# A Mamba scan on Trainium2: the product with C written one column to the left of the states, and the carried state copied later by ScalarE instead of GpSimd

## Chip, core and metric

The kernel runs on one core of one Trainium2 chip. The metric is the device time of one execution in microseconds (us); lower is better. The engines are named as in the profile: PE is TensorE's matmul, PEld its weight load, DVE is VectorE, ACT is ScalarE, POOL is GpSimd, and SP is SyncE, whose queue issues the DMAs.

## What is computed

The input `x` is 8 samples of 512 channels by 48 x 48 = 2304 positions. Layer 0 is a causal linear attention with 8 heads, layer 1 splits the 512 channels into four blocks of 128 and runs a Mamba block on each, one after the other, since block i gets the result of block i-1 added to its input. The change lies in the recurrence of the Mamba block:

```python
delta = softplus(dt @ Wdt.T + bdt)
A = -exp(A_log)                                   # 256 channels x 16 states
dA = exp(einsum('bld,dn->bldn', delta, A))
dBu = einsum('bld,bln->bldn', delta * xs, Bm)
def step(h, inp):
    dA_t, dBu_t, C_t = inp
    h = dA_t * h + dBu_t
    return (h, einsum('bdn,bn->bd', h, C_t))      # y_t = sum over the states of h * C
```

So for every channel and state there is a first-order recurrence along the 2304 positions, and the states are then multiplied by C and summed over the 16 states. Around it stand projections, a convolution over four positions, two gates with silu, a skip `xs * Dp`, and a fusion of input and output by maxima and means. Everything is in float32.

## The kernel before

**Tiling.** A sample's block is a *stream block*; it is cut along the positions into NC = 6 chunks of LC = 384. One chunk of one block is a `Job`; there are 192. Two streams, even and odd samples, take turns in the order of the list `turns`, so that one stream's block boundary falls beside the other's work. The 128 partitions hold 64 channels times two states. A job has eight *slots*: half of the channels (`h = s // 4`) times four pairs of states, and a slot has four scans of 384 columns each (`NG` = 2 state groups times 2 channel groups). There are 1536 slots.

**One slot.** All of a slot's data is in one tile `u` of shape 128 x 2 x 2 x 385, out of five that go round (`bufs=5`). In each of its four rows, column 0 takes the state carried in from the chunk before, and columns 1 to 384 hold first the products B times `delta * xs` and then, in place, the states. The steps, with the lines that the profile names:

- `last_product` (L856, POOL) takes a tile `u` and writes the products of its last 128 columns; ahead of it ScalarE copies the carried state from `state` into column 0 (L855). It is issued at the middle of a slot for the slot two later.
- `product` (L867, DVE) writes the first 256 columns from `dxp`, a copy in PSUM that `inputs` (L840, ACT) makes. It is issued at a slot's start for the next slot.
- `decay` (L877, ACT) writes `exp(delta * A)` into a PSUM bank. Decays run up to `DEPTH` = 3 ahead of the scans; six banks are shared with the attention and the projections.
- `scan` (L888, DVE) runs the recurrence on one row of `u`, in place, and frees the decay's bank.
- `weigh` (L902 and L904, POOL), after the four scans: it first copies the last column, that is the state to be carried to the next chunk, into the small tile `state` (not in the last chunk, hence 1280 times), and then multiplies columns 1 to 384 in place by C.
- `gather` (L911, PE) adds the products up over the states by four matmuls into `yp` in PSUM. It is issued at the middle of the slot after next, from the list `waiting`.
- `skip` (L845, ACT) writes `xs * Dp` into `yp` before a half's gathers, and `gated` (L923, DVE) multiplies the finished half by the gate into `yz`.

**What else the engines do.** The attention of the next samples (`chunk`: projections L293, features L305 and L306, `q` L350, `k` L358), the preparation of the next jobs (`prepare`: convolution L693, silu, softplus L764, `delta * xs` L805), statistics and the passing on of a block's result (`pass_on`: `fu` L662, `xi` L667, `xo` L670) run as *tasks* between the scans. `delta * xs` overwrites `delta` in place, so it waits until `delta` has been stored for the broadcast of `dr`.

**What sets the order.** The whole program is written under `manual_schedule`: each engine executes its instructions in the order in which the Python code issues them, and a wait at the head of an engine's queue holds everything behind it. Function `slot` issues a slot's work; its middle is the point after the second scan (`i == 1`). Tasks carry due times in half slots and are stepped by `beside`.

Of the kernel before, what the change touches and what calls it, by code (L numbers as in the profile page):

```python
# [12 lines left out]
ALU = mybir.AluOpType  # L13
# [4 lines left out]
P = 128  # L18
T = 128
LC = 384  # L20
NG = 2
# [29 lines left out]
def attention_then_mamba_kernel(  # L51
# [17 lines left out]
    nc = tc.nc  # L69
# [94 lines left out]
    def flush(every=True):  # L164
        while stores and (every or stores[0][0] <= half_no[0] - 2):
            _, o, i = stores.pop(0)
            nc.sync.dma_start(out=o, in_=i)
# [506 lines left out]
    class Job:  # L674
# [222 lines left out]

        def weigh(self, s, u):

            h, q = s // 4, s % 4 * NG  # L900
            if self.c + 1 < NC:
                nc.gpsimd.tensor_copy(self.state[:, h, q : q + NG, :], u[:, :, :, LC])  # L902
            h = u[:, :, :, 1:]
            nc.gpsimd.tensor_tensor(  # L904
                h, h, self.C[s % 4].unsqueeze(2).to_broadcast([P, NG, 2, LC]), ALU.mult
            )

        def gather(self, s, u):
            for j in range(NG):
                for g in range(2):  # L910
                    nc.tensor.matmul(  # L911
                        self.yp[g * 64 : g * 64 + 64, 0:LC],
                        pair_sum,
                        u[:, j, g, 1:],
                        start=False,
                        stop=(s % 4 == 3 and j == NG - 1),
                        skip_group_check=True,
                    )
# [96 lines left out]
    def finale(job):  # L1015
        yield "0", 1
        job.project()
        yield "1", 0
        job.maximum()
        if job.c == NC - 1:  # L1020
            yield from job.stream.pass_on()
# [29 lines left out]
    def beside(half):  # L1051

        half_no[0] = half
        flush(every=False)
        begin(half // 2 + LEAD)

        for t in heads:
            if t.need is not None and t.need[1] == 0 and t.fits() and t.due():
                t.step()
        held = False  # L1060
        for t in tasks + heads:
            while t.need is not None and t.due():
                if not t.fits() or held and t.need[1]:
                    held = held or t.need[1] > len(spare)
                    break
                t.step()
        prune()

    def hurry(k, ready):

        for _ in range(1000):
            flush()
            begin(k)
            if ready():
                break
            moved = False
            for t in heads + tasks:
                if t.need is not None and t.fits() and (t.start <= k and t in tasks or t.due()):
                    need = t.need
                    t.step()  # L1080
                    moved = moved or t.need != need or need[0] != "1w"
            if not moved:
                half_no[0] += 1
            prune()
        assert ready()

    def at(k):
        return jobs[k // SLOTS], k % SLOTS

    def apart(k):  # L1090

        return k % SLOTS == 0 and k > 0 and at(k)[0].c == 0 and at(k)[0].stream is at(k - 1)[0].stream

    us, decays, waiting = {}, [], []
    todo = 0
    primed, drawn = set(), set()

    def ahead(n):

        nonlocal todo  # L1100
        while len(decays) < n and spare and todo < 4 * slots:
            k = todo // 4
            if apart(k) and k not in primed:
                break
            job, s = at(k)
            if not job.prepared or s // 4 not in job.dr:
                break
            decays.append(job.decay(s, todo % 4))
            todo += 1

    def close(k):

        job = at(k)[0]
        while waiting:
            waiting.pop(0)()
        job.gated(1)
        job.closed = True
        tasks.insert(0, Task(finale(job)))

    def prime(k):  # L1120
        job, s = at(k)
        hurry(k, lambda: job.prepared)
        primed.add(k)
        job.inputs(0)
        for r in range(2):
            us[k + r] = job.last_product(s + r)
        job.product(s, us[k])
        ahead(DEPTH)

    def slot(k):  # L1130
        job, s = at(k)
        end = k + 1 == slots or apart(k + 1)
        if not end and k + 1 not in drawn:
            j, r = at(k + 1)
            j.product(r, us[k + 1])
        before = jobs[k // SLOTS - 1] if k >= SLOTS else None
        if s == 2 and before is not None and not before.closed:
            before.gated(1)
            tasks.insert(0, Task(finale(before)))
        elif s == 6:  # L1140
            job.gated(0)
        beside(2 * k)
        for i in range(4):
            job.scan(s, i, us[k], decays.pop(0))
            if i == 0 and s in (2, 6):
                job.skip(s // 4)
            ahead(DEPTH)
            if i == 1:

                if len(waiting) > 1:  # L1150
                    waiting.pop(0)()
                if s == 2:
                    job.inputs(1)
                elif s == 6 and k + 2 < slots and not apart(k + 2):
                    j = at(k + 2)[0]
                    if not j.prepared:
                        hurry(k + 2, lambda: j.prepared)
                    j.inputs(0)
                if not end and k + 2 < slots and not apart(k + 2):
                    j, r = at(k + 2)  # L1160
                    us[k + 2] = j.last_product(r)
                    if s == 7:

                        j.product(r, us[k + 2])
                        drawn.add(k + 2)
                beside(2 * k + 1)
        u = us[k]
        job.weigh(s, u)
        waiting.append(lambda: at(k)[0].gather(s, us.pop(k)))
        if end:  # L1170
            close(k)
            if k + 1 < slots:
                prime(k + 1)
            else:
                hurry(slots, lambda: not tasks)
                flush()

    with tc.manual_schedule():
        half_no[0] = FIRST - 6
        Task(statistics(0)).finish()  # L1180
        for st in streams:
            tasks.append(Task(st.weights()))
            tasks.append(Task(st.pass_on()))
        for half in range(FIRST - 6, 0):
            beside(half)
        prime(0)
        for k in range(slots):
            slot(k)
# [70 lines left out]
```

## Time and profile before

| | |
|---|---|
| Median of 3 runs | 8786.02 us (8785.19 to 8791.31) |
| Span of the profiled execution, first to last instruction | 8790.1 us; its time beyond the span is not listed apart |
| Instructions in the profile | 122,627 |
| Mean granted TensorE clock | 0.964 |
| DMA: share of 16 engines, rate | about 70%, mean 187 GB/s |
| POOL COPY `state<-u` (L902) | 1280 times, 242.4 us |
| POOL TENSOR_TENSOR `u<-u,C` (L904) | 1536 times, 4882.7 us, mean 3179 ns |
| DVE scans (L888) | 6144 times, 5457.0 us, mean 939 ns |
| ACT decays (L877) | 6144 times, 3413.6 us, mean 578 ns |

How to read it: the page's first part gives each engine's busy time and its share of the span. The costliest groups have, after the bar, the busy time of a group, the mean time of one instruction, and the idle time of the engine just before the group's instructions with what ended it. The waits say who waited for whom: total us, number of times, longest. The chain of waits follows the work that ended last back from the end, at each step to what released it. The timeline gives start and duration of each instruction in us; equal neighbours are merged ("x2").

### The profile page before, as it was taken

The numbers are of one execution on the slowest core, as the hardware profiler recorded it, in microseconds if no ns is written. First come the engines' busy times: TensorE is split into PE (matmuls) and PEld (weight loads), VectorE is DVE, ScalarE is ACT, GpSimd is POOL, SyncE is SP. The second block draws the span as 40 slices with busy tenths as digits, with TensorE's granted clock in tenths as the row PEclk, the third lists the DMA queues.
The fourth block names the chain that finished last, engine by engine and source line by source line (L and its number), as shares of the span: only waits on it lengthen the run. The fifth ranks groups of instructions, "written<-read, shape, count | busy, mean of one in ns | idle before, by whom it ended". The sixth has DMA issues, their size and how long they took to land.

```text
span 8790.1 us, 122627 instructions
## 1 busy us (share of the span) xinstructions
PE 7766.8 (88%) x36482; PEld 3705.4 (42%) x36482; DVE 8067.0 (92%) x11078; ACT 6744.5 (77%) x13220; POOL 8044.8 (92%) x5623
## 2 busy tenths in 40 slices
PE   7899999998899899998889999999888999999865
PEld 4444444444444444444444444444444444444422
DVE  2899999999899999998889999999889999999998
ACT  2777887777788878777778878877777888877875
POOL 1789999999999999999999999999999999999998
PEclk9999999999999999999999999999999999999977
DMA  5667777766676777776667677777667666766655
GB/s 184 166 174 189 193 197 195 190 188 186 190 191 188 191 195 198 196 190 189 179 190 192 188 191 198 198 195 188 188 183 191 189 187 187 189 187 185 183 156 144
DMA packets 1002907, 1642.98 MB, mean 187 GB/s; under 512 B 138592, under 2 KB 797312, under 8 KB 1002240
## 3 DMA queue, kind: packets, MB, share of 16 engines
q1 hardware_dynamic: 1002240, 1635.13, 69.0%
q8 instruction: 291, 4.77, 0.2%
q14 instruction: 376, 3.08, 0.1%
HBM read 1309.06 MB, written 325.58 MB: 186 GB/s over the span
## 4 chain that ended last, share of the span: by engine, by line
DVE 28%; POOL 20%; ACT 14%; DMA 13%; PE 13%; issue 7%; SPq 4%; POOLq 0%; DVEq 0%; ACTq 0%
DVE u L888 19%; POOL u L904 11%; ACT bank L877 5%; DVE u L867 5%; POOL u L856 4%; PE bank L693 4%; PE bank L293 3%; PE yp L911 3%; DMA C<-scr 3%; SPq L797 2%; DMA dscr<-delta 2%; ACT L877 2%; DMA B<-scr 1%; ACT L764 1%; POOL delta L805 1%
## 5 line engine op out<-in xcount | busy, mean ns | idle before, releaser
L888 DVE TENSOR_TENSOR_SCAN u<-bank,u 128x385 f32<-128x385 f32 (+1 forms) x6144 | 5457.0, 939 | 350.1 <-ACT bank L877 300.3
L904 POOL TENSOR_TENSOR u<-u,C 128x1536 f32<-128x1536 f32 x1536 | 4882.7, 3179 | 121.9 <-DVE gm_m L182 16.9
L877 ACT ACTIVATE bank<-dr,av 128x385 f32<-128x385 f32 (+1 forms) x6144 | 3413.6, 578 | 752.3 <-DVE u L888 611.9
L911 PE MATMUL yp<-u,cst 128*64 128x384 f32 x12288 | 2440.7, 519 | 428.2 <-POOL u L904 355.9
L856 POOL TENSOR_TENSOR u<-B,dxr 128x512 f32<-128x512 f32 x1536 | 1960.9, 1277 | 16.5 <-DMA dxr<-xscr 13.8
L867 DVE TENSOR_TENSOR u<-B,dxp 128x1024 f32<-128x1024 f32 x1536 | 1836.0, 1195 | 11.3 <-ACT dxp L840 11.1
L293 PE MATMUL bank<-xn,wq_sb 128*128 128x384 f32 x4608 | 1680.1, 508 | 82.2 <-POOL xn L317 40.1
L911 PEld LDWEIGHTS yp<-u,cst 128*64 128x64 f32 x12288 | 782.0, 140 | 1660.6 <-issue 842.6
L693 PE MATMUL bank<-xi,wk 128*128 128x384 f32 x3072 | 1117.8, 507 | 218.5 <-ACT kl L390 112.5
L293 PEld LDWEIGHTS bank<-xn,wq_sb 128*128 128x128 f32 x4608 | 849.0, 195 | 826.5 <-DVE u L888 119.6
L693 PEld LDWEIGHTS bank<-xi,wk 128*128 128x128 f32 x3072 | 560.6, 192 | 780.8 <-ACT kl L390 202.1
L805 POOL TENSOR_TENSOR delta<-delta,xs 128x384 f32<-128x384 f32 x384 | 384.4, 1001 | 278.0 <-DMA dscr<-delta 215.9
L305 ACT ACTIVATE ex<-bank,bqkv_sb 128x384 f32<-128x384 f32 x384 | 221.0, 576 | 523.8 <-PE bank L293 523.6
L877 ACT ACT_TABLE_LOAD x382 | 490.1, 1283 | 6.7
L845 ACT ACTIVATE yp<-xs,pv 128x384 f32<-128x384 f32 x384 | 223.8, 583 | 290.8 <-DVE yz L923 289.3
L902 POOL COPY state<-u 128x4 f32<-128x4 f32 x1280 | 242.4, 189 | 172.6 <-DVE u L888 170.0
L753 PE MATMUL bank<-dbc,wd 9*128 9x384 f32 x768 | 315.6, 532 | 1.2 <-ACT dbc L745 1.1
L929 PE MATMUL bank<-yz,wo 128*128 128x384 f32 x768 | 299.2, 506 | 18.5 <-DVE yz L923 14.6
L704 PE MATMUL bank<-xi,wi 128*128 128x384 f32 x768 | 285.9, 494 | 10.9 <-ACT xs L729 10.9
L740 PE MATMUL bank<-xs,wx 128*40 128x384 f32 x768 | 281.0, 489 | 2.6 <-ACT sm L457 2.6
L923 DVE TENSOR_TENSOR yz<-yp,sz 128x384 f32<-128x384 f32 x384 | 211.6, 551 | 62.5 <-PE yp L911 62.3
L423 PE MATMUL bank<-cst,rdb 128*128 128x128 f32 x576 | 113.0, 311 | 170.7 <-DVE u L888 168.5
(117 smaller groups left out, 8018.7 us busy)
## 6 DMA issues: line engine op xcount, KB each, us to landing
B<-scr SPq DMA_DIRECT2D x1536, 192.0 KB
C<-scr SPq DMA_DIRECT2D x1536, 192.0 KB
xn<-xn SPq DMA_DIRECT2D x192, 768.0 KB
dr<-dscr SPq DMA_DIRECT2D x768, 192.0 KB
dxr<-xscr SPq DMA_DIRECT2D x768, 192.0 KB
dscr<-delta SPq DMA_DIRECT2D x192, 384.0 KB
xscr<-delta SPq DMA_DIRECT2D x192, 384.0 KB
xn<-in_x SPq DMA_DIRECT2D x48, 768.0 KB
```

Source lines behind the costliest of these rows:

```text
L293: nc.tensor.matmul(ps, wq_sb[:, kt, j * 512 + o * P : j * 512 + (o + 1) * P], xn[:, kt, :], start=(kt == 0), stop=(kt == 3),)
L693: nc.tensor.matmul(xc, wk[:, k, h * P : (h + 1) * P], xi[:, c0 + k : c0 + k + LC], start=(k == 0), stop=(k == 3),)
L704: nc.tensor.matmul(zp, wi[:, 256 + h * P : 256 + (h + 1) * P], xi[:, c0 + 3 : c0 + 3 + LC], start=True, stop=True,)
L753: nc.tensor.matmul(vp, wd[32:41, h * P : (h + 1) * P], dbc[32:41, :], start=True, stop=True)
L805: nc.gpsimd.tensor_tensor(delta[:, h, :], delta[:, h, :], xs[:, h, :], ALU.mult)
L856: nc.gpsimd.tensor_tensor(u[:, :, :, 1 + LC - TAIL :], self.B[s % 4][:, :, cols].unsqueeze(2).to_broadcast(shape), self.dxr[s // 4][:, :, ...
L867: nc.vector.tensor_mul(u[:, :, :, 1 : 1 + LC - TAIL], self.B[s % 4][:, :, cols].unsqueeze(2).to_broadcast(shape), self.dxp.unsqueeze(1).to ...
L877: nc.scalar.activation(dA[:, cols], self.dr[h][:, g, cols], AF.Exp, scale=self.w[6][:, 2 * h + g, q + j : q + j + 1],)
L888: nc.vector.tensor_tensor_scan(u[:, j, g, cols], dA[:, cols], u[:, j, g, cols], 0.0, ALU.mult, ALU.add,)
L904: nc.gpsimd.tensor_tensor(h, h, self.C[s % 4].unsqueeze(2).to_broadcast([P, NG, 2, LC]), ALU.mult)
L911: nc.tensor.matmul(self.yp[g * 64 : g * 64 + 64, 0:LC], pair_sum, u[:, j, g, 1:], start=False, stop=(s % 4 == 3 and j == NG - 1), skip_gro ...
L929: nc.tensor.matmul(self.xm[:, 0:LC], self.w[2][:, h, :], self.yz[:, h, :], start=(h == 0), stop=(h == 1),)
```

## The change

Three things are changed. `weigh` still multiplies columns 1 to 384 by C, but writes the result to columns 0 to 383, so the last column keeps the raw state. `gather` reads from columns 0 to 383. The copy of the last column into `state` leaves `weigh` and GpSimd; it is a function of its own, `keep`, on ScalarE, put into a list `kept` at the end of a slot and issued at the middle of the next slot, ahead of everything else that is issued there (or in `close`, where a run of slots ends).

```diff
         def weigh(self, s, u):
 
+            nc.gpsimd.tensor_tensor(
+                u[:, :, :, 0:LC],
+                u[:, :, :, 1:],
+                self.C[s % 4].unsqueeze(2).to_broadcast([P, NG, 2, LC]),
+                ALU.mult,
+            )
+
+        def keep(self, s, u):
+
             h, q = s // 4, s % 4 * NG
             if self.c + 1 < NC:
-                nc.gpsimd.tensor_copy(self.state[:, h, q : q + NG, :], u[:, :, :, LC])
-            h = u[:, :, :, 1:]
-            nc.gpsimd.tensor_tensor(
-                h, h, self.C[s % 4].unsqueeze(2).to_broadcast([P, NG, 2, LC]), ALU.mult
-            )
+                nc.scalar.copy(self.state[:, h, q : q + NG, :], u[:, :, :, LC])
...
                         pair_sum,
-                        u[:, j, g, 1:],
+                        u[:, j, g, 0:LC],
                         start=False,
...
-    us, decays, waiting = {}, [], []
+    us, decays, waiting, kept = {}, [], [], []
...
     def close(k):
 
         job = at(k)[0]
+        while kept:
+            kept.pop(0)()
         while waiting:
             waiting.pop(0)()
...
             if i == 1:
 
+                while kept:
+                    kept.pop(0)()
                 if len(waiting) > 1:
                     waiting.pop(0)()
...
         job.weigh(s, u)
+        kept.append(lambda: at(k)[0].keep(s, u))
         waiting.append(lambda: at(k)[0].gather(s, us.pop(k)))
```

## Prediction

> **What bounds the kernel now.** I read the busy shares first, then the waits of each engine, then one job at a time, then the chain of waits. The busy line:
>
> ```profile
> PE 7766.8 (88%) x36482; PEld 3705.4 (42%) x36482; DVE 8067.0 (92%) x11078; ACT 6744.5 (77%) x13220; POOL 8044.8 (92%) x5623
> ```
>
> Two engines, DVE and POOL, are level, and each is idle for some 720 to 745 us of the span. Cut by jobs (eight slots), the stretches differ. In a quiet job both are almost full; in a disturbed one neither is. The windows of busy time (columns: us, then PE, PEld, DVE, ACT, POOL) of one job of each kind:
>
> ```profile
> 3177.00:3222.00 45.00, 38.97 (x190) 18.62 (x190) 42.43 (x58) 36.17 (x74) 39.38 (x31) 1.00 0.76 201
> 3313.40:3355.70 42.30, 39.12 (x194) 18.78 (x193) 41.77 (x57) 35.02 (x70) 41.03 (x29) 1.00 0.71 188
> ```
>
> The quiet job takes 42.3 us with 41.8 of DVE work: DVE sets it, and nothing done to POOL can shorten it. But POOL works 41.0 of the 42.3 us, so it has almost no reserve to catch up when something has held it. What holds it, and who waits later, is in the waits (us, times, longest):
>
> ```profile
> POOL delta L805 <- DMA dscr<-delta: 215.9, 93, 25.9
> POOL state L902 <- DVE u L888: 170.0, 152, 13.9
> ```
>
> ```profile
> DVE u L888 <- ACT bank L877: 300.3, 212, 4.4
> DVE q L350 <- ACT bank L306: 102.4, 57, 6.0
> DVE yz L923 <- PE yp L911: 62.3, 39, 6.6
> DVE u L888 <- POOL u L856: 49.0, 41, 2.9
> ```
>
> The second line of POOL's waits carries most: only 152 of 1280 state copies found POOL waiting for DVE's scans, so in the other 88% POOL was behind. Measured slot by slot in the timeline, `weigh` starts a median 2.55 us after the slot's last scan ends. The disturbed job shows the mechanism in POOL's timeline (start, us):
>
> ```profile
> 3190.09 1.27 POOL L856 TENSOR_TENSOR u<-B,dxr 128x512 f32<-128x512 f32 x1
> 3196.33 1.00 POOL L805 TENSOR_TENSOR delta<-delta,xs 128x384 f32<-128x384 f32 x1 [4.97 <-DMA dscr<-delta]
> 3197.28 0.18 POOL L902 COPY state<-u 128x4 f32<-128x4 f32 x1
> 3197.54 3.17 POOL L904 TENSOR_TENSOR u<-u,C 128x1536 f32<-128x1536 f32 x1
> ...
> 3214.46 1.27 POOL L856 TENSOR_TENSOR u<-B,dxr 128x512 f32<-128x512 f32 x1
> ```
>
> and, in DVE's,
>
> ```profile
> 3215.76 1.81 DVE L888 TENSOR_TENSOR_SCAN u<-bank,u 128x385 f32<-128x385 f32 x2 [1.44 <-POOL u L856]
> ```
>
> A multiply waits 5 us for a store, POOL then works without a gap, and 19 us later DVE stands 1.44 us for POOL's `last_product`.
>
> **What the Trainium skill says.** GPSIMD Engine Reference, section 2.1, says that completion gates what waits on an instruction's semaphore but does not hold back the next Pool instruction. The trace agrees: POOL instructions follow each other with a gap of about -0.05 us, but `weigh`, which waits for the copy before it, starts 0.08 us after that copy's end. ScalarE: Activation LUTs, section "Table sets", says that copies are in every set, so that a copy needs no table load: the 1280 copies of L855 have none. The same page, "What ACT_TABLE_LOAD costs", says that back-to-back activations overlap by about 93 ns. The trace shows 60 to 105 ns.
>
> **The change part by part.**
>
> 1. *POOL loses 1280 copies (L902).* The row, and its twin on ACT that shows the price there:
>
> ```profile
> L902 POOL COPY state<-u 128x4 f32<-128x4 f32 x1280 | 242.4, 189 | 172.6 <-DVE u L888 170.0 <-DVE gm_a L181 0.5
> L855 ACT COPY u<-state 128x4 f32<-128x4 f32 x1280 | 238.6, 186 | 5.7 <-PE yp L911 3.0
> ```
>
> With a copy, `last_product` starts 1.217 us before the copy and the copy 0.269 before `weigh` (medians), in all 1.486. In the last chunk of a stream, where no copy is made, `last_product` to `weigh` is 1.230 (151 cases). So a copy takes 0.256 us of POOL, more than its 0.189: 1280 x 0.256 = 328 us of engine time. In the changed program `weigh` waits for its scans and for `last_product` of its own tile, long done; the wait instructions that this adds to POOL's queue cost nothing in the trace (same gaps behind none, one or two of them) while POOL is behind.
>
> 2. *What of it is on the path.* Followed piece by piece, the chain of waits crosses 304 copies, 47.4 us, and 16.2 us of idle time between copy and what follows: 64 us, the most that this chain can give. The disturbed job gives a second estimate: three copies lie between the stall's end (3196.33) and the late `last_product` (3214.46), 3 x 0.256 = 0.77 of 1.44 us. About six jobs in each round of twelve lose 3 to 5 us over DVE's own work, with 16 rounds: 96 x 0.77 = 74 us. The two agree. Not all of it arrives: PE (88%) must still work off its queue, the store that holds the delta multiply doesn't move, and DVE is full in the quiet jobs. I take 40 us, some six tenths of 64; the bounds are 0 and 64.
>
> 3. *ACT gains 1280 copies.* Price from L855: where ACT is busy, L855 starts 0.507 us after the decay before it, as a next decay would, and the next decay 0.084 us after L855's start (low quartile of 662 cases). So each adds about 0.085 us to a busy ACT, 109 us in all, and 0.19 us each at most. ACT is idle a fifth of the time, and that hides most of it. If the cover is gone, decays (L877) queued behind it come late and DVE's scans wait. L855, which stands beside the new copy in ACT's queue, is on the chain 158 times: 158 x 0.085 = 13 us. Against that, of the 347 times that DVE waits on ACT, only two follow an unbroken run of ACT work with an L855 copy in it. I take 7 us, bounds 0 and 30 (158 x 0.19).
>
> 4. *New waits.* The copy waits for `last_product` and the scans of its own tile, all finished half a slot before, and not for `weigh`: the columns don't overlap. What is queued behind it on ACT (L855, then decays) is not held. `last_product` of five slots later must wait for the copy to have read the tile; DVE's scans between them need decays queued behind that copy, so it has always run. SP's queue keeps its order, and no DMA moves.
>
> 5. *The product one column to the left.* Same count, shape and reads; 384-column multiplies whose output starts three columns in (xi L667, 1.001 us) and at column 0 (xo L670, 1.005) cost the same, so I take 0. The gather reads from column 0 instead of 1: convolution matmuls at four different column offsets (L693, 0.507 us) cost what aligned ones do (L293, 0.508): 0. Both could be off either way, since no shifted overlap of input and output is in the trace: plus or minus 0.1 us of a product is 1536 x 0.1 = 154 us of POOL, of which a fifth (983 of 4883 us of L904 are on the chain) or 31 us is felt.
>
> Sum: -40 + 7 = -33 us from the span 8790.1, or 8757. The three runs have a median of 8786.0, 4 us below the profiled span, so the median after would be about **8753**.
>
> **The rivals.** What this kernel's measurement can tell from no change is about 0.2%, 17.6 us.
>
> - *The relief does not reach the end* (0.20). POOL merely waits longer for the store and for DVE: the delta waits grow from 216 us, DVE's idle time stays near 723. For it: the quiet jobs, 99% DVE. Against it: DVE waits that name POOL or the gathers behind it (49 + 62 us). Time 8778 to 8790.
> - *ScalarE becomes the bound* (0.10), the one that ends slower. The copy stands ahead of the decays at mid-slot, and the waits of scans on L877 (300 us, the largest of DVE) grow. With 40 us of relief it decides from 40 / 0.085 = 470 exposed copies, 37% of all, against the 158 of the trace. If all are exposed: 109 - 40 = +69, 8855.
> - *The shifted product is slower* (0.06): break-even on POOL is 328 / 1536 = 0.21 us a product (7%). At +0.3 us the chain's fifth gives 94 - 40 = +54, 8840. Against it: point 5.
> - That POOL's order stays as it was is ruled out: the changed program has 1280 fewer POOL instructions, the same 1280 more on ACT, and otherwise one order on every engine.
>
> **How the numbers follow.** Forecast (0.64): 8753. Low end: all 64 us and no cost give 8722; 22 us more for a product a little faster or copies that the inferred chain misses: 8700. High end 8812: the slower cases begin at 8804, and the range takes in their start. Faster 0.64, same 0.20, slower 0.16.
>
> **What would show it.** Right: L902 is gone from POOL, POOL busy falls by about 242 us to 7800, `weigh` stays at 3179 ns; POOL's waits for DVE's scans become far more than 152; DVE's waits on L856 and on the gathers (111 us together) fall by half or more; the ACT copy has a mean of 0.19 us and almost no idle time before it; DVE's wait on L877 stays within 300 to 330 us. Wrong: L877's wait grows by over 40 us (ScalarE), or `weigh` exceeds 3.25 us (shift), or DVE's idle time is unchanged while POOL's grows by the whole 328 us (no path).

## The result, and the profile after

The changed kernel took 8720.0 us (median of 4 runs, 8712.5 to 8725.8) against 8788.7 us (median of 4 runs). The recorded ratio is 0.9914 with a 95% interval of 0.9902 to 0.9927; at 8789 us that is 76 us faster, between 64 and 86. The medians alone give 69 us. A second measurement of both kernels (e11 below) gives 75 us by its medians; the record has the same ratio and interval for it to the last digit, so the two ratios are not taken as independent. The profiled execution took 8723.1 us, with a span of 8721.0. The forecast was 33 us faster: the direction was right and the time lies in the range, but the gain is more than twice what was forecast.

The busy line of the page after:

```profile
PE 7774.7 (89%) x36482; PEld 3714.5 (43%) x36482; DVE 8072.2 (93%) x11078; ACT 6852.0 (79%) x14500; POOL 7834.3 (90%) x4343
```

POOL has 1280 instructions fewer and is busy 210 us less, ACT has 1280 more and is busy 108 us more. DVE has the same work, so the gain is idle time of DVE: 723 us of the span before, 649 after.

The waits of POOL, of DVE and (the line before is shown with it) of PE after:

```profile
POOL delta L805 <- DMA dscr<-delta: 234.6, 80, 24.4
POOL u L900 <- DVE u L888: 186.9, 92, 14.5
```

```profile
DVE u L888 <- ACT bank L877: 288.3, 213, 4.5
DVE q L350 <- ACT bank L306: 69.5, 69, 6.0
...
DVE yz L928 <- PE yp L916: 41.0, 28, 5.8
DVE u L888 <- POOL u L856: 38.7, 34, 2.9
```

```profile
PE yp L911 <- POOL u L904: 355.9, 293, 4.4
```

```profile
PE yp L916 <- POOL u L900: 259.6, 149, 5.2
```

The two waits of DVE that name POOL or the gathers (L856, `yz`) fell from 111 to 80 us, and `q` by 33 us, from 102 to 70 (77 in e11). By the program's order `q` waits for ACT's features, which wait for PE's projections, which stand in PE's queue behind the gathers; and PE's waits for the product fell by 96 us. So POOL's lateness seems to reach DVE by more ways than the two that name it. The experiments below bear this out: with more POOL work DVE's wait at `q` is 125 us (e3), and with the work given back 108 us (e9). The wait on decays (L877), where a dearer ScalarE would show, did not grow. Slot by slot in the timeline, `weigh` now starts a median 1.64 us after the last scan instead of 2.55.

The same stretch of POOL's timeline as before, after the same stall:

```profile
3168.05 1.00 POOL L805 TENSOR_TENSOR delta<-delta,xs 128x384 f32<-128x384 f32 x1 [5.92 <-DMA dscr<-delta]
3169.01 3.18 POOL L900 TENSOR_TENSOR u<-u,C 128x1536 f32<-128x1536 f32 x1
...
3185.41 1.27 POOL L856 TENSOR_TENSOR u<-B,dxr 128x512 f32<-128x512 f32 x1
```

From the stall's end to the `last_product` that DVE waits for it takes 17.36 us, 18.13 before: 0.77 less, the price of three copies as forecast. The stall itself is still there. DVE's wait behind it is now 0.61 us, where it was 1.44:

```profile
3186.72 1.81 DVE L888 TENSOR_TENSOR_SCAN u<-bank,u 128x385 f32<-128x385 f32 x2 [0.61 <-POOL u L856]
```

Yet this job takes 44.5 us in both kernels, and the one that became shorter is the next (columns as in the prediction, then the granted clock; before, then after):

```profile
3221.90:3268.60 46.70, 44.53 (x195) 21.34 (x195) 42.10 (x59) 35.28 (x72) 44.97 (x26) 0.89 0.76 194
```

```profile
3193.20:3235.70 42.50, 39.06 (x192) 19.13 (x191) 41.84 (x58) 35.42 (x73) 42.50 (x24) 1.00 0.71 187
```

In that next job DVE waited 2.5 us at `q` and 1.1 us at `yz` before, and at neither after. That looks like a late product costing time a job later, where no wait of DVE names POOL; one stretch doesn't show that it is the rule. The granted clock was lower in that job before, but over the whole span it is 0.964 in both, so it doesn't explain the gain as a whole. Counted over the traces, from first scan to first scan, DVE is idle for over 3 us in 63 of 191 jobs before, and in 39 after (43 in e11).

And the rows of the two ScalarE copies and of the product (after the bar: busy us, mean ns, then the idle time before):

```profile
L855 ACT COPY u<-state 128x4 f32<-128x4 f32 x1280 | 247.6, 193 | 0.9 <-ACT state L911 0.2
L911 ACT COPY state<-u 128x4 f32<-128x4 f32 x1280 | 235.5, 184 | 6.4 <-DVE u L888 2.7 <-POOL u L900 1.3
```

```profile
L900 POOL TENSOR_TENSOR u<-u,C 128x1536 f32<-128x1536 f32 x1536 | 4892.7, 3185 | 345.6 <-DVE u L888 186.9 <-issue 39.9 <-DMA B<-scr 31.6
```

The new copy holds ACT up for 6 us in all. The product takes 3185 ns instead of 3179; `last_product`, which was not changed, went from 1277 to 1283 likewise, so no price of the shift's own is seen.

### The profile page after: what moved, and what is told of

It reads as the page before. It is cut to its first block, busy times and chain, and to the rows that moved or that the text cites. A ratio compares the mean times of both kernels' runs of the same rounds, so it can differ in the third digit from the quotient of the medians.

```text
span 8721.0 us, 124881 instructions
## 1 busy us (share of the span) xinstructions
PE 7774.7 (89%) x36482; PEld 3714.5 (43%) x36482; DVE 8072.2 (93%) x11078; ACT 6852.0 (79%) x14500; POOL 7834.3 (90%) x4343
## 5 line engine op out<-in xcount | busy, mean ns | idle before, releaser
L900 POOL TENSOR_TENSOR u<-u,C 128x1536 f32<-128x1536 f32 x1536 | 4892.7, 3185 | 345.6 <-DVE u L888 186.9
L877 ACT ACTIVATE bank<-dr,av 128x385 f32<-128x385 f32 (+1 forms) x6144 | 3405.1, 578 | 671.0 <-DVE u L888 575.2
L856 POOL TENSOR_TENSOR u<-B,dxr 128x512 f32<-128x512 f32 x1536 | 1969.9, 1283 | 17.5 <-DMA dxr<-xscr 15.4
L293 PE MATMUL bank<-xn,wq_sb 128*128 128x384 f32 x4608 | 1725.8, 519 | 74.2 <-DVE u L888 33.0
L293 PEld LDWEIGHTS bank<-xn,wq_sb 128*128 128x128 f32 x4608 | 867.4, 199 | 842.4 <-DVE u L888 140.0
L877 ACT ACT_TABLE_LOAD x382 | 490.1, 1283 | 6.8
L476 PE MATMUL bank<-sm,v 128*64 128x128 f32 x2304 | 257.1, 302 | 0.0
L729 ACT ACT_TABLE_LOAD x192 | 246.3, 1283 | 3.6 <-PE bank L693 0.2
```

The costliest lines, as they stand in the source:

```text
L293: nc.tensor.matmul(ps, wq_sb[:, kt, j * 512 + o * P : j * 512 + (o + 1) * P], xn[:, kt, :], start=(kt == 0), stop=(kt == 3),)
L856: nc.gpsimd.tensor_tensor(u[:, :, :, 1 + LC - TAIL :], self.B[s % 4][:, :, cols].unsqueeze(2).to_broadcast(shape), self.dxr[s // 4][:, :, ...
L877: nc.scalar.activation(dA[:, cols], self.dr[h][:, g, cols], AF.Exp, scale=self.w[6][:, 2 * h + g, q + j : q + j + 1],)
L900: nc.gpsimd.tensor_tensor(u[:, :, :, 0:LC], u[:, :, :, 1:], self.C[s % 4].unsqueeze(2).to_broadcast([P, NG, 2, LC]), ALU.mult,)
```

## The experiments

Each ratio is against the kernel before, run beside it, with its 95% interval. Microseconds are the ratio's distance from 1 times 8789. Two experiments of four or five runs whose ratios differ by less than about 0.0018, or 16 us, are not told apart; this is an estimate from the intervals below.

Theory: GpSimd's time, wherever it stands in its queue, reaches the end at some rate (microseconds of run time for each microsecond of GpSimd's time), since GpSimd works off a backlog in most slots; the copies on ScalarE are nearly hidden. Rivals: the gain is the product's earlier start behind the scans, not GpSimd's time; or the ScalarE copies cost much and the gain beneath is larger still.

**e1: no copy at all.** The carried state is set to zero once for each block and never written again.

```diff
-                nc.scalar.copy(self.state[:, h, q : q + NG, :], u[:, :, :, LC])
+                pass
...
+            nc.gpsimd.memset(self.state, 0.0)
```

> The changed kernel with the copy of the last column left out: `state` is set to zero once a block and never written again, so no state is carried from chunk to chunk. ScalarE has 1280 instructions fewer (109 us at 0.085 us each), GpSimd 32 memsets more. If the copies on ScalarE are hidden, this is within 5 us of the changed kernel (8715 to 8722, ratio to before 0.991 to 0.992). If they cost the 7 us that the prediction took, or up to the 30 us of its bound, it is faster by that: 8713 down to 8690 (0.9885).

Measured: 0.9908 (0.9893 to 0.9923), 81 us faster than before, 5 us more than the changed kernel, and not to be told apart from it. What 1280 copies cost on ScalarE is small.

**e4: a second copy on ScalarE.**

```diff
                 nc.scalar.copy(self.state[:, h, q : q + NG, :], u[:, :, :, LC])
+                nc.scalar.copy(junk, u[:, :, :, LC])
```

> The changed kernel with a second copy of the last column on ScalarE, into a small tile that nobody reads: 1280 x 0.085 = 109 us more for ScalarE. If copies at that place are hidden: 8718 to 8725 (0.992). If each on the chain counts (158 x 0.085 = 13 us): 8733 (0.9935). If ScalarE is near to becoming the bound: over 8750 (0.9955).

Measured: 0.9934 (0.9922 to 0.9947), 58 us faster than before, 18 us less than the changed kernel; the intervals overlap a little. The middle expectation (13 us) is nearest. With e1, a set of 1280 copies on ScalarE costs some 5 to 18 us, of which the 5 can't be told from nothing; the prediction took 7.

**e2: the shifted product alone, the copy still on GpSimd.**

```diff
         def weigh(self, s, u):
+            h, q = s // 4, s % 4 * NG
+            if self.c + 1 < NC:
+                nc.gpsimd.tensor_copy(self.state[:, h, q : q + NG, :], u[:, :, :, LC])
             nc.gpsimd.tensor_tensor(
                 u[:, :, :, 0:LC],
...
-                nc.scalar.copy(self.state[:, h, q : q + NG, :], u[:, :, :, LC])
+                pass
```

> The product one column to the left, but the copy of the state stays on GpSimd ahead of the product. The product no longer overwrites what the copy reads, so it doesn't wait for it: a copy should take 0.13 us of GpSimd (0.189 less the overlap of 0.05) in place of 0.256. If GpSimd's time is what counts, at the rate of the changed kernel (69 us for 328 us given back, 0.21 us each us), 161 us given back give 34 us: 8753, ratio 0.996. If the wait between copy and product was all, 8720 (0.992). If only the copy's leaving GpSimd counts, 8787 (1.000). If the shift itself slowed the product, above 8787.

Measured: 0.9948 (0.9935 to 0.9960), 46 us faster. In its timeline the product starts 0.146 us after the copy's start, 0.269 before: the wait between them is gone, and with it 0.123 us a copy, 157 us of GpSimd. So some six tenths of the gain (46 of 76 us) come without moving the copy, only because the product no longer overwrites what the copy reads. The rate is 46 / 157 = 0.29, above the 0.21 that I had expected.

**e3: the kernel before with a second copy on GpSimd.**

```diff
+                nc.gpsimd.tensor_copy(junk, u[:, :, :, LC])
                 nc.gpsimd.tensor_copy(self.state[:, h, q : q + NG, :], u[:, :, :, LC])
```

> The kernel before with a second copy of the last column, into a small tile that nobody reads, ahead of the first on GpSimd: 1280 x 0.13 = 170 us more for GpSimd. If the time falls and rises with GpSimd's time at 0.21 us each us: 8823 (1.004). If GpSimd is close to being the bound in the quiet jobs (41.0 of 42.3 us before, 41.9 with the second copy), the rate rises to a half: 8870 (1.010). If GpSimd's time doesn't count: 8787.

Measured: 1.0067 (1.0055 to 1.0080), 59 us slower, for 1280 x 0.127 = 163 us: a rate of 0.36 (0.30 to 0.43 by the interval), between the two expectations.

**e9: GpSimd's time given back in another place.** The changed kernel, with two copies at mid-slot that nobody reads, after the product and ahead of `last_product`.

```diff
                 nc.scalar.copy(self.state[:, h, q : q + NG, :], u[:, :, :, LC])
+                nc.gpsimd.tensor_copy(junk, u[:, :, :, LC])
+                nc.gpsimd.tensor_copy(junk_2, u[:, :, :, LC])
```

> The changed kernel with two copies of the last column, into two small tiles that nobody reads, given back to GpSimd, but at mid-slot after the product and ahead of the next last_product: 1280 x 2 x 0.13 = 333 us, what the change had taken off GpSimd. If GpSimd's time is what counts, wherever in its queue it stands, this loses what the change gained: 8790 to 8805 (1.000 to 1.002), the ScalarE copies included. If the gain came from the product starting right behind the scans, little of it is lost, as each product in a gap still starts at once: 8720 to 8745 (0.992 to 0.995).

Measured: 1.0022 (1.0014 to 1.0029). All of the gain is gone, and 19 us more: 95 us lost against the changed kernel. The rate at the expected price of 333 us is 95 / 333 = 0.29. No product waits for these copies of its own slot. So it is GpSimd's time that counts and not where in the slot the copy stood. The rival of the earlier start has fallen. The 19 us are about what e4 gives for the copies on ScalarE, which this kernel has and the one before has not.

**e8: the copy on ScalarE at the slot's end, the product still in place**, so that GpSimd must wait for ScalarE.

```diff
-                nc.gpsimd.tensor_copy(self.state[:, h, q : q + NG, :], u[:, :, :, LC])
+                nc.scalar.copy(self.state[:, h, q : q + NG, :], u[:, :, :, LC])
```

> The kernel before with the copy on ScalarE at the slot's end, and the product in place, so that the product on GpSimd must wait for ScalarE's copy. GpSimd gives back the same 328 us. If GpSimd is behind in most slots, the copy has been made by the time that it gets to the product, and this is close to the changed kernel: 8720 to 8740 (0.992 to 0.994). If ScalarE is often late at that place, GpSimd and with it the gathers wait: 8790 or more (1.000), and the product's idle time before it grows by over 300 us.

Measured: 0.9942 (0.9930 to 0.9955), 51 us faster, at the upper edge of the first expectation. GpSimd's waits in it name the new wait first:

```profile
POOL u L904 <- ACT state L902: 408.7, 256, 15.5
```

Some of these would have been waits for the scans: the idle time before the product is 513 us in all, 346 in the changed kernel. e7, which follows, has the copy at the same early place on ScalarE, but with the shift, and is as fast as the changed kernel. So with the copy at this place the shift is worth 25 us: without it, GpSimd gives back its time but waits for ScalarE.

**e7: the shift, but no delay of half a slot.**

```diff
-        kept.append(lambda: at(k)[0].keep(s, u))
+        job.keep(s, u)
```

> The changed kernel with ScalarE's copy issued at the slot's end in place of half a slot later: it then waits on ScalarE for the slot's last scan, ahead of the decays. If the decay behind it would have waited for a bank from that scan anyway, it costs at most 10 us over the changed kernel: 8720 to 8730 (0.992 to 0.993). If the half slot is needed, ScalarE stands at the copy and DVE's waits on decays (288 us) grow by a third or more: 8800 or more (1.001).

Measured: 0.9913 (0.9900 to 0.9927), the same as the changed kernel. The copy now waits 191 us on ACT:

```profile
L877 ACT ACTIVATE bank<-dr,av 128x385 f32<-128x385 f32 (+1 forms) x6144 | 3404.7, 579 | 623.1 <-DVE u L888 516.5 <-DVE S L415 87.5 <-DVE gm_a L195 3.7
L911 ACT COPY state<-u 128x4 f32<-128x4 f32 x1280 | 243.1, 190 | 191.0 <-DVE u L888 167.4 <-POOL u L856 6.4 <-POOL u L900 5.0
```

But ACT's idle time as a whole is the span less its busy time, 8704.8 - 6869.8 = 1835 us, against 8721.0 - 6852.0 = 1869 in the changed kernel, where the decays alone waited 671 us: what ACT waits at the copy, it no longer waits at the decays and elsewhere. DVE's waits on L877 are 282 us in it, 288 in the changed kernel. The "half a slot later" of the change does nothing for the time that can be told here.

**e5 and e6: less of the stall.** The in-place delta multiply is due one half slot later, in the kernel before (e5) and in the changed one (e6).

```diff
             for h in range(2):
-                yield "1", 0
+                yield "21"[h], 0
                 nc.gpsimd.tensor_tensor(delta[:, h, :], delta[:, h, :], xs[:, h, :], ALU.mult)
```

> The kernel before, with the in-place delta multiply (L805) due one half slot later, so that the store that it waits for has mostly landed; the multiplies stand later in GpSimd's queue, and with them the store of delta * xs. If the 216 us of waits there are where GpSimd's backlog begins, most of them go and DVE's waits on last_product and on the gathers fall: at 0.3 us each us some 50 us faster, 8745 (0.994). If the later store makes dxr late, the waits of last_product on it and of dxp grow: slower, 8810 or more (1.002). If the stall only moved to another wait: 8790 (1.000).

> The changed kernel with the same later delta multiply. If backlog from the stall and backlog from the copies add up, it gains about as much as it does in the kernel before: 8670 (0.986). If the copies' removal has already given GpSimd the reserve to absorb the stall, it gains little: 8710 to 8720 (0.991). If dxr gets late: 8740 or more (0.994).

Measured: e5 0.9853 (0.9840 to 0.9867), 129 us faster than before; e6 0.9814 (0.9801 to 0.9828), 8626 us, 164 us faster than before and the fastest of all. I had expected 44 and about 119. The wait of the multiply, in e5 and in e6:

```profile
POOL delta L805 <- DMA dscr<-delta: 54.9, 18, 25.4
```

```profile
POOL delta L805 <- DMA dscr<-delta: 65.9, 23, 27.8
```

and what is left in e5 of DVE's waits that name GpSimd or the gathers (111 us before):

```profile
DVE yz L923 <- PE yp L911: 12.3, 10, 4.9
...
DVE u L888 <- POOL u L856: 9.2, 9, 2.3
```

So these stalls (93 waits for the store before, 18 in e5) are where much of the lateness that reaches DVE begins. They are not its only source: in e5 `weigh` still starts a median 1.97 us after the last scan, 2.55 before. All idle time in front of the multiply fell from 278 to 66 us for the 129 us gained, a rate of 0.61, so a microsecond of these stalls costs about twice what one of the copies does. With most of them gone, the change is worth 0.0039 or 34 us (e5 against e6), less than half of what it is worth with them. The waits on `dxr`, where the price of the delay would show, did not grow: 22 us before, 21 in e5.

**e10: two half slots later** (`"31"[h]`), the changed kernel otherwise.

> The changed kernel with the delta multiply due two half slots later in place of one. If the store's landing is still what is waited for with one (66 and 79 us of waits on it are left there), a bit faster still than with one: 8605 to 8620 (0.980). If the later store of delta * xs now makes dxr late, the gain turns: 8640 or more (0.983), with waits of last_product or dxp on DMA dxr.

Measured: 1.1037 (1.1022 to 1.1052), 911 us slower than the kernel before. The late `dxr` that I named as the other side is there, far larger than I had put it. ACT's longest wait and DVE's two longest:

```profile
ACT dxp L840 <- DMA dxr<-xscr: 856.6, 144, 10.5
```

```profile
DVE u L867 <- ACT dxp L840: 807.5, 136, 9.5
DVE u L888 <- ACT bank L877: 561.6, 203, 4.9
```

The store of delta * xs and the broadcast load behind it have no slack for a second half slot. SP's queue, which issues both, stands 2030 us for the multiply in e10 (1187 in the changed kernel), and the loads of `dr`, for the decays, and of `dxr` are issued behind it. Each late load then stands at the head of ScalarE's queue, and 136 times it stops DVE, for 5.9 us on average; DVE's waits for decays rose too, from 288 to 562 us.

**e11: the changed kernel again.**

> The changed kernel once more, as it is, beside the others on one chip: 8715 to 8725 against 8789, ratio 0.991 to 0.993. The half slot of delay, the second copies and the left-out copies are read against this run's ratio.

Measured: 8711.2 us, the median of 5 runs, against 8786.1; recorded ratio 0.9914 (0.9902 to 0.9927), the same entry as in the result above.

## Why the prediction was right or wrong

- **What bounds the kernel: right.** DVE full in the quiet jobs, GpSimd without reserve, losses after GpSimd's stalls. e5 shows it from the other end: with the stalls mostly gone, DVE's waits for `last_product` and the gathers fall from 111 to 22 us.
- **A copy takes 0.256 us of GpSimd, 328 us in all: right.** e2 and e3 give 0.123 us for the wait and 0.127 for the copy itself, in sum 0.25.
- **How much of it is felt, 40 us: wrong; this is the term that was mis-sized.** The measured gain of 69 to 76 us, with the 5 to 18 us that ScalarE's copies cost, is 74 to 94 us: a rate of 0.23 to 0.29, where I had taken 40 / 328 = 0.12. e2 (0.29), e9 (0.29) and e3 (0.36) give rates near it by other ways. Two choices made it small. The 64 us called the most that the chain can give counted only the pieces of the 304 copies that the chain showed (47.4 us) and the idle time behind them (16.2 us), 0.21 us each; at the price of 0.256 from the same step they are 78 us, and the estimate by jobs said 74. (That this one came so near is in part luck: it took 96 jobs that lose 3 to 5 us, and the trace has 63 in which DVE is idle for over 3 us.) And the cut to six tenths had no measured figure behind it. The three reasons given for it did not hold back the gain: PE's waits for the product fell by 96 us, and DVE's idle time by 74 us, where the span of the profile lost 69. Why the gain can exceed 78 us, as the upper figures have it, stays open; one inferred chain is not a bound. With most of the stalls gone the rate is lower: in e5 against e6 it is 34 us, or 39 to 52 with ScalarE's copies, of 328, that is 0.12 to 0.16. So the share that I forecast is near that of a kernel without the stalls.
- **ScalarE's copies, 7 us: right in size** (5 and 18 us in e1 and e4), and the copy has only 6 us of idle time before it.
- **The half slot: costed at nothing, right**, though the half slot wasn't needed to avoid a cost: in e7 the wait at the slot's end only takes the place of other waits of ACT.
- **The shift, 0 us for the instruction: right.** But it is not without effect: it takes away a wait, in e2 for GpSimd's own copy, in e8 for ScalarE's.
- **The signs to look for:** POOL's busy time fell by 210, not 242, mainly as the other POOL instructions' records grew by some 6 ns; L877 stayed; DVE's waits for L856 and the gathers fell by 28%, not by half; and the waits of POOL that the list of waits puts down to scans fell from 152 to 92, where I had expected more. That list gives each wait to whatever ended last, and the product's idle time now goes under many names (345.6 us, of which 186.9 for scans; the copy had 172.6). Counted in the traces, POOL was idle just before the first instruction after a slot's scans 204 times before and 370 times after, of 1536, so what the sign was meant to show did come. Most of the rest of DVE's gain came through `q`.
- **The rivals:** of "does not reach the end", "ScalarE becomes the bound" and "the shifted product is slower", none occurred.

## What to carry to other kernels

When an engine works off a backlog in most rounds, price its small instructions by start-to-start distance, waits included, and make no cut for "something else will absorb it" without a measured figure; a doubled or displaced dummy instruction (e3, e9) measures the rate at which such time is felt. The rate is not a constant: it was 0.12 to 0.16 with the stalls mostly gone and 0.36 with more work on GpSimd. Before moving work off such an engine, look for what stalls it: here a change of one due time gained more (129 us) than the moved copies (76 us), and the two overlap. A due time has a cliff on its other side, so move it a step at a time: one half slot later gave the fastest kernel here, two were 10% slower than the kernel before.

## What the runs showed of the hardware

In the kernel before, the product, which waits for the GpSimd copy just before it, starts 0.08 us after that copy's end; in e2, where it does not wait, it starts about 0.05 us ahead of the end (0.269 against 0.146 us from copy to product, medians of 1280). For a copy with a record of 0.19 us, the wait costs 0.123 us, about as much as the copy itself (0.127 us start to start, e3).

On ScalarE, small copies cost less than their records say: in the changed kernel a copy that follows another starts 0.086 us after the first one's start (770 cases), though each has a record of 0.19 us.
